# Delta stored in pieces of 256 positions and loaded two chunks at a time by the selective scan, with projection weights held only in their phase

## Chip, core and metric

The kernel runs on one core of one Trainium2 chip. The metric is the device time of one execution in microseconds (us). Before the change three runs took 11842.54, 11845.06 and 11851.63 us; the median is 11845.06 us. Two times within about 0.2% of each other can't be told apart here.

## What is computed

The input holds 8 images of 96 channels by 64 x 64 positions (L = 4096). Layer 0 is a layer norm, an input projection to 192 + 192 channels, a depthwise 3 x 3 convolution with SiLU, and then a selective scan along four orders of the positions (k = 0..3: by rows, by columns, and both backwards). Layer 1 is a linear attention and a feed-forward block. The change concerns the scan and what feeds it:

```python
x_dbl = jnp.einsum('bkdl,kcd->bkcl', xs, x_proj_w)
dts, Bs, Cs = jnp.split(x_dbl, [DTRANK, DTRANK + DSTATE], axis=2)
dts = jnp.einsum('bkrl,kdr->bkdl', dts, dt_proj_w)
delta = jax.nn.softplus(dts + dt_proj_b[None, :, :, None])
...
def step(h, t):
    u_t, d_t, B_t, C_t = t
    dA = jnp.exp(d_t[..., None] * A)
    h = dA * h + (d_t * u_t)[..., None] * B_t[:, :, None, :]
    y = jnp.einsum('bkdn,bkn->bkd', h, C_t)
    return (h, y)
```

For each k, delta is a softplus of a rank-6 projection, one number for each of 192 channels and each position; the state h has 16 numbers per channel.

## The kernel before

The images go in four pairs. Two images of 192 channels are 384 rows, held as three tiles T of 128 rows (T = 2 takes 64 rows of each image). For each pair there are three phases, and the back end of one pair runs beside the front end of the next:

1. `project` (norms, input projection), `convolve` and `gates` (SiLU, line 354) leave the scan's input `xi` in on-chip memory. Beside them run `back` and `tail` of the pair before, which end in the stores `out<-ot` (line 859).
2. `prepare` (lines 365 to 432) goes through two orders o of the positions, 8 chunks c of F = 512 positions, and the two k of each order: 32 rounds, in which the text calls one (o, c, k) a round. A round makes `pt` by three matmuls with `xw` (line 392), copies it to `S` (ScalarE, line 396), and stores the rows of B and C (`bs`, `cs`, line 398). For each T it then makes `pq` by a matmul with `dtw` (404), delta by a softplus (ScalarE, 408), `du` = delta x u (VectorE, 412), and splits delta into three bf16 parts that together hold its float32 value: part 0 on ScalarE (424), the rest on VectorE (425), part 1 on ScalarE (426), part 2 on GpSimd (427). `du` and the parts `dp` are stored to DRAM through `spread` (lines 359 and 362: one DMA for T < 2, two for T = 2). The tiles `S`, `delta`, `du`, `dp` and `rest` have three buffers each. For o = 1, GpSimd first copies `xi` into transposed tiles `u` (line 384, two buffers).
3. `scan` (lines 435 to 666) goes through 128 steps, four k with 32 chunks of TC = 128 positions. Its order is written out by hand. In step s, visit v (0 to 7), TensorE makes the exponents `da` from the delta parts `dm` and weights `aw` (`decay`, 570), two visits ahead; ScalarE takes their exp (577); GpSimd makes `dbu` = du x B (552); VectorE runs the scan (588); TensorE sums over states (606). `load(s + 1)` fetches the delta parts of the next step at visit 0, in two DMAs (478, 479) of 576 and 192 KB, whose rows are 6144 bytes.

Every DMA is issued from the one queue of SyncE (SP), in order; a DMA that must wait holds those behind it. Outside the scan a scheduler sets the order on each engine. Delta lies in DRAM as `dl`, bf16, laid out as [k][chunk of 128][part][16 rows m][24 entries e][128 positions], so that a store writes runs of 128 x 2 = 256 bytes; `du`, float32 with the same chunk, is written in runs of 512 bytes. The projection weights `winT` (input projection), `xw` and `dtw` are loaded once, at the start, into tiles that stay for the whole kernel. The lines at issue:

```python
dl: [KD, NT, 3, 16, NE, TC]                      # L889, bf16
dp = tmp.tile([128, F // TC, 3, TC], BF16)       # L419
dm[s] = wk.tile([128, NE, TC], BF16, name="dm")  # L475, two buffers
v = dl[k, c].rearrange("a m e t -> (a m) (e t)")
nc.sync.dma_start(to[0:96], v.unsqueeze(1).to_broadcast([48, 2, NE * TC]))
nc.sync.dma_start(to[96:128], v[0:32])
```

Of the kernel before, what the change touches and what calls it, by code (L numbers as in the profile page):

```python
# [19 lines left out]
DIM = 96  # L20
DI = 192
# [16 lines left out]
HQ = TC // 4  # L38
NE = 24
X0 = F - 3 * SEG  # L40
LOGEXP = "natural_log_exp_and_others"


# [8 lines left out]
def vss_attn_ffn(ctx: ExitStack, tc: tile.TileContext, a: dict):  # L52
# [33 lines left out]

    nw = load("nw", [DIM, 1])
    nb = load("nb", [DIM, 1])
    winT = load("winT", [DIM, 2 * DI])
    inb = const.tile([128, 2], F32, name="inb")  # L90
    nc.sync.dma_start(inb, a["inb"][:, 0])
    convw = load("convw", [128, 2, 9])
# [1 line left out]
    dtb = load("dtb", [128, KD, 2])  # L94


    xw = const.tile([128, KD, 3, 76], F32, name="xw")
    dtw = const.tile([128, KD, 3, 128], F32, name="dtw")
    with tc.tile_pool(name="xprep", bufs=2) as wp:
        for k in range(KD):  # L100
            for g in range(2):
                xg = wp.tile([128, 3, 2 * NS], F32, name="xg")
                nc.sync.dma_start(xg, a["xw"][k, :, g, :, 0:32])
                for b in range(2):
                    o = 32 * g + NS * b
                    nc.vector.tensor_copy(
                        xw[:, k, :, o : o + NS].rearrange("p t (n z) -> p t n z", z=2),
                        xg[:, :, NS * b : NS * b + NS].rearrange("p t (z n) -> p t n z", z=2),
                    )
            nc.sync.dma_start(xw[:, k, :, 64:76], a["xw"][k, :, 0, :, 32:44])  # L110
            nc.sync.dma_start(dtw[64:76, k], a["dtw"][k])

    def cut(name, v, *rest):

# [123 lines left out]
    def project(pair, zs, ybuf, p1, tmp, ps):  # L238

        pad = [t.rearrange("p (h w) -> p h w", w=HH + 2) for t in ybuf]  # L240
        for t in ybuf:
            nc.gpsimd.memset(t, 0.0)
        for b in range(2):
            xt = p1.tile([DIM, L], F32, name="xt", bufs=2)
            nc.sync.dma_start(xt, x[2 * pair + b])
            bst = tmp.tile([DIM, NCH, 6], F32, name="bst")
            for c in range(NCH):
                nc.vector.bn_stats(bst[:, c, :], xt[:, bass.ts(c, F)])
            mv = tmp.tile([DIM, 2], F32, name="mv")
            nc.vector.bn_aggr(mv, bst.rearrange("p c s -> p (c s)"))  # L250
            gps = ps.tile([128, F], F32, name="gps", tag="fps")
            nc.tensor.matmul(gps[:DIM, 0:1], gmat, mv[:, 0:1], start=True, stop=True)
            gm = tmp.tile([DIM, 1], F32, name="gm")
            nc.vector.tensor_copy(gm, gps[:DIM, 0:1])
            gd = tmp.tile([DIM, 1], F32, name="gd")
            nc.vector.tensor_tensor(gd, mv[:, 0:1], gm, ALU.subtract)
            gv = tmp.tile([DIM, 1], F32, name="gv")
            nc.vector.scalar_tensor_tensor(gv, gd, gd, mv[:, 1:2], ALU.mult, ALU.add)
            vps = ps.tile([128, F], F32, name="vps", tag="fps")
            nc.tensor.matmul(vps[:DIM, 0:1], gmat, gv, start=True, stop=True)  # L260
            gr = tmp.tile([DIM, 1], F32, name="gr")
            rsqrt(gr, vps[:DIM, 0:1])
            yield
            nc.vector.tensor_scalar(xt, xt, gm, gr, ALU.subtract, ALU.mult)

            for c in range(NCH):
                cs = bass.ts(c, F)
                cps = ps.tile([128, F], F32, name="cps", tag="fps")
                nc.tensor.matmul(cps[:DIM], c96, xt[:, cs], start=True, stop=True)
                sq = tmp.tile([DIM, F], F32, name="sq", bufs=1)  # L270
                nc.scalar.activation(sq, cps[:DIM], AF.Square)
                vp = ps.tile([128, F], F32, name="vp", tag="fps")
                nc.tensor.matmul(vp[:DIM], j96, sq, start=True, stop=True)
                rs = tmp.tile([DIM, F], F32, name="rs", bufs=1)
                rsqrt(rs, vp[:DIM])
                nc.vector.tensor_tensor(xt[:, cs], cps[:DIM], rs, ALU.mult)
                nc.vector.tensor_scalar(xt[:, cs], xt[:, cs], nw, nb, ALU.mult, ALU.add)
                yield

            lo = slice(64 * b, 64 * b + 64)  # L280
            for c in range(NCH):
                cs = bass.ts(c, F)
                r0 = c * ROWS
                pm = ps.tile([128, F], F32, name="pm", tag="fps")
                nc.tensor.matmul(pm, winT[:, 0:128], xt[:, cs], start=True, stop=True)
                nc.scalar.activation(
                    pad[b][:, r0 + 1 : r0 + 1 + ROWS, 1 : HH + 1],
                    pm.rearrange("p (h w) -> p h w", w=HH),
                    AF.Identity, bias=inb[:, 0:1],
                )  # L290
                pl = ps.tile([128, F], F32, name="pl", tag="fps")
                nc.tensor.matmul(pl[lo], winT[:, 128:DI], xt[:, cs], start=True, stop=True)
                nc.scalar.activation(
                    pad[2][lo, r0 + 1 : r0 + 1 + ROWS, 1 : HH + 1],
                    pl[lo].rearrange("p (h w) -> p h w", w=HH),
                    AF.Identity, bias=inb[lo, 1:2],
                )
                zt = tmp.tile([DIM, 2, F], F32, name="zt")
                for g in range(2):
                    pz = ps.tile([128, F], F32, name="pz", tag="fps")  # L300
                    nc.tensor.matmul(
                        pz[:DIM], winT[:, DI + g * DIM : DI + (g + 1) * DIM], xt[:, cs],
                        start=True, stop=True,
                    )
                    table("silu", lambda: nc.scalar.activation(
                        zt[:, g], pz[:DIM], AF.Silu, bias=inz[:, g]
                    ))
                nc.sync.dma_start(zs[b, :, :, cs].rearrange("g p l -> p g l"), zt)
                yield
# [55 lines left out]
    def prepare(xi, us, dl, du, bs, cs_):  # L365
        with ExitStack() as st:
            tmp = st.enter_context(tc.tile_pool(name="p2", bufs=3))
            ps = st.enter_context(tc.tile_pool(name="p2ps", bufs=3, space=PSUM))
            pd = st.enter_context(tc.tile_pool(name="p2pd", bufs=4, space=PSUM))

            for T in range(3):
                spread(lambda o, n: us[o : o + n], T, xi[T])
            dlv = dl.rearrange("k c a m e t -> k c a (m e) t")
            duv = du.rearrange("k c m e t -> k c (m e) t")
            for o in range(2):
                for c in range(NCH):
# [12 lines left out]
                    for k in (o, o + 2):  # L389
# [12 lines left out]
                        for T in range(3):  # L402
# [13 lines left out]
                                T, q.rearrange("p (j t) -> p j t", t=TC),  # L416
                            )

                            dp = tmp.tile([128, F // TC, 3, TC], BF16, name="dp")  # L419
                            rest = tmp.tile([128, F], F32, name="rest")  # L420
                            d, rest = [
                                t.rearrange("p (j t) -> p j t", t=TC) for t in (d, rest)
                            ]
                            nc.scalar.activation(dp[:, :, 0], d, AF.Copy)  # L424
                            nc.vector.tensor_tensor(rest, d, dp[:, :, 0], ALU.subtract)  # L425
                            nc.scalar.activation(dp[:, :, 1], rest, AF.Copy)  # L426
                            nc.gpsimd.tensor_tensor(dp[:, :, 2], rest, dp[:, :, 1], ALU.subtract)  # L427
                            spread(
                                lambda o, n: dlv[k, j, :, o : o + n]
                                .rearrange("j a p t -> p (j a) t"),  # L430
                                T, dp.rearrange("p j a t -> p (j a) t"),
                            )
# [2 lines left out]
    def scan(dl, du, bs, cs_, ys):  # L435
        with ExitStack() as st:
# [33 lines left out]
            def load(s):  # L470

                if s >= N:
                    return
                k, c, _ = steps[s]
                dm[s] = wk.tile([128, NE, TC], BF16, name="dm")  # L475
                v = dl[k, c].rearrange("a m e t -> (a m) (e t)")
                to = dm[s].rearrange("p e t -> p (e t)")
                nc.sync.dma_start(to[0:96], v.unsqueeze(1).to_broadcast([48, 2, NE * TC]))
                nc.sync.dma_start(to[96:128], v[0:32])

            def load_bc(s):
# [79 lines left out]
            def decay(p):  # L561

                if p >= 8 * N:
                    return
                s, v = divmod(p, 8)
                r, z = divmod(v, 2)
                k = steps[s][0]
                e = da[p % 3][:, 0:W6].rearrange("p (i u) -> p i u", u=SEG)[:, :, 1:]
                for i in range(NI):
                    nc.tensor.matmul(  # L570
                        e[:, i], aw[k, r][:, i, z, :], dm[s][:, NI * r + i, :],
                        start=True, stop=True,
                    )
                if p == 0:
                    table("ln", lambda: nc.scalar.activation(e, e, AF.Exp))
                else:
                    nc.scalar.activation(e, e, AF.Exp)  # L577
# [49 lines left out]
            for r in range(NR):  # L627
                load_aw(0, r)
            load(0)
            fetch(0)  # L630
            for _ in load_bc(0):
                pass
# [9 lines left out]
            for s in range(N + 2):  # L642
                for v in range(8):
# [8 lines left out]
                            sums(s - 1, f)  # L652
                    if s < N:
                        if v == 0:
                            load(s + 1)
                        if v == 1:
                            fetch(2 * s + 3)
                        if v == 5:
# [224 lines left out]
    for pair in range(npair + 1):  # L883

        new = {}
        if pair < npair:
            for name, shape, dtype in (
                ("zs", [2, 2, DIM, L], F32), ("us", [2 * DI, L], F32),
                ("dl", [KD, NT, 3, 16, NE, TC], BF16), ("du", [KD, NT, 16, NE, TC], F32),  # L889
                ("bs", [KD, NT // NB, 2 * NS, NB * TC], F32),  # L890
                ("cs", [KD, NT // NB, 2 * NS, NB * TC], F32), ("ys", [KD, 16, L, NE], F32),
                ("t1", [2, DIM, L], F32), ("tn", [2, DIM, L], F32),
# [161 lines left out]
```

## Time and profile before

| what | value |
|---|---|
| median of three runs | 11845.06 us |
| the profiled execution | 11820.4 us, its span 11818.4 us |
| mean granted TensorE clock | 0.816 |
| VectorE busy, share of the span | 8756.4 us, 74% |
| GpSimd | 7986.7 us, 68% |
| TensorE matmuls | 8675.0 us, 73% |
| ScalarE | 6900.1 us, 58% |
| data DMA: packets, bytes, share of 16 engines | 1654228, 2068.13 MB, 75.4% |
| DMA packets under 512 bytes | 962179 of 1655919 |
| first scan starts of the four pairs (line 588) | 638.8, 3533.6, 6431.7 and 9333.5 us |

The profile is one execution, recorded on the chip. In rows of a group, busy time comes first, then the mean or the min/median/max of one instruction, then the idle time of the engine ahead of it with what ended it (the releaser). A DMA packet is one contiguous run that a DMA engine moves; "share" is the mean busy share of the core's 16 DMA engines. PEclk is the clock that TensorE was granted, as a part of the full one. A float32 matmul of one source line is two TensorE instructions. The kernel repeats one pattern four times, once a pair, with the phases one after the other; shares over the whole span are an average over phases with different limits.

### The profile page before, as it was taken

The page shows a single profiled execution, that of the slowest core. Times are in us where ns is not written, and L with a number is a line of the kernel's source. Part 1 is how long each engine was busy: PE and PEld are TensorE (multiplying, and loading weights), DVE is VectorE, ACT ScalarE, POOL GpSimd, SP SyncE. Part 2 cuts the span into 40 slices and gives each one's busy share as a digit, 9 for nine tenths or more (in the row PEclk, how much of TensorE's full clock was granted, in tenths as well). Part 3 has the DMA queues.
Part 4 walks back from the last instruction along what each step waited for, and adds up shares of the span by engine and source line. Part 5 has one row for each costly group of instructions (what it writes and reads, how often), then busy time and mean ns, then how long its engine had stood idle before and what let it go on. Part 6 is the DMA issues. An engine that isn't in the chain of part 4 may idle for free. (4 is left out here: it accounts for less than half of the span.)

```text
span 11818.4 us, 387513 instructions
## 1 busy us (share of the span) xinstructions
PE 8675.0 (73%) x170112; PEld 5662.7 (48%) x170112; DVE 8756.4 (74%) x6465; ACT 6900.1 (58%) x12176; POOL 7986.7 (68%) x2770
## 2 busy tenths in 40 slices
PE   7856666779877666667986666667898666667787
PEld 2245555544225555554422555555442355555542
DVE  5489999963549999995355999999454699999922
ACT  3556666644456666664455666666445566666623
POOL 0489999960249999994025999999313699999910
PEclk8678888879768888888976888888896788888896
DMA  2988888875398888886459888888646988888862
GB/s 79 215 198 201 198 203 201 198 160 134 97 215 195 203 201 200 204 195 149 120 125 209 197 202 199 197 199 199 148 99 156 203 199 199 200 198 200 193 132 63
DMA packets 1655919, 2092.92 MB, mean 177 GB/s; under 512 B 962179, under 2 KB 1307348, under 8 KB 1651412
## 3 DMA queue, kind: packets, MB, share of 16 engines
q1 hardware_dynamic: 1654228, 2068.13, 75.4%
q8 instruction: 1335, 21.87, 0.9%
q14 instruction: 356, 2.92, 0.1%
HBM read 1604.17 MB, written 463.54 MB: 175 GB/s over the span
## 5 line engine op out<-in xcount | busy, mean ns | idle before, releaser
L588 DVE TENSOR_TENSOR_SCAN h<-da,dbu 128x774 f32<-128x774 f32 x4096 | 7028.4, 1760 | 646.5 <-ACT da L577 443.1
L552 POOL TENSOR_TENSOR dbu<-dut,bc 128x1536 f32<-128x1536 f32 x2048 | 7083.1, 3506 | 578.1 <-ACT dbu L549 478.7
L577 ACT ACTIVATE da<-da 128x768 f32<-128x768 f32 x4092 | 3254.2, 797 | 2155.9 <-PE da L570 2117.6
L606 PE MATMUL yp<-h,cw 128*32 128x48 f32 x131072 | 3145.2, 246 | 1126.0 <-issue 1110.7
L570 PE MATMUL da<-dm,aw 128*128 128x128 bf16 x24576 | 2502.0, 251 | 1447.2 <-DVE h L588 1098.1
L606 PEld LDWEIGHTS yp<-h,cw 128*32 128x32 f32 x131072 | 2548.9, 155 | 1673.2 <-issue 1408.7
L570 PEld LDWEIGHTS <-aw 128*128 128x128 bf16 x24576 | 1844.5, 111 | 1774.5 <-issue 1452.5
L506 ACT ACTIVATE cw<-bc,blk 128x512 f32<-128x512 f32 x2048 | 1472.8, 720 | 297.9 <-DMA bc<-cs 216.2
L745 POOL TENSOR_TENSOR yk<-yk 128x768 f32<-128x768 f32 x64 | 115.8, 1809 | 1268.2 <-DMA yk<-ys 1010.6
L427 POOL TENSOR_TENSOR dp<-rest,dp 128x512 bf16<-128x512 f32 x384 | 458.1, 1194 | 707.3 <-ACT dp L426 691.6
L425 DVE TENSOR_TENSOR rest<-delta,dp 128x512 f32<-128x512 f32 x384 | 301.1, 785 | 628.2 <-ACT dp L424 628.2
L404 PE MATMUL pq<-S,dtw 12*128 12x512 f32 x768 | 594.8, 882 | 140.2 <-ACT delta L408 75.3
L614 ACT ACTIVATE yev<-yp 128x384 f32<-128x384 f32 x1024 | 503.4, 492 | 243.1 <-PE yp L606 240.6
L858 POOL TENSOR_TENSOR ot<-t,y 96x512 f32<-96x512 f32 x64 | 128.1, 2002 | 612.0 <-DVE y L856 593.7
L786 DVE SCALAR_TENSOR_TENSOR g<-yc,c_onw,yrs 96x512 f32<-96x512 f32 x128 | 89.9, 742 | 483.2 <-ACT yrs L190 483.2
L404 PEld LDWEIGHTS pq<-S,dtw 12*128 12x128 f32 x768 | 162.4, 250 | 566.0 <-ACT delta L408 179.1
L426 ACT ACTIVATE dp<-rest 128x512 bf16<-128x512 f32 x384 | 241.6, 630 | 327.3 <-DVE rest L425 327.3
L672 ACT ACTIVATE nsq<-ncp 96x512 f32<-96x512 f32 x128 | 75.8, 592 | 572.8 <-PE ncp L670 559.6
L549 ACT COPY dbu<-h 128x12 f32<-128x12 f32 x1984 | 407.1, 205 | 0.0
L758 PEld LDWEIGHTS py<-ident,yk 128*24 128x24 f32 x8192 | 231.6, 108 | 241.7 <-issue 182.6
L758 PE MATMUL py<-ident,yk 128*24 128x128 f32 x8192 | 319.1, 290 | 31.5 <-DVE yk L744 25.7
L384 POOL COPY u<-xi 128x512 f32<-128x512 f32 x96 | 109.3, 1156 | 327.6 <-ACT xi L354 296.6
(136 smaller groups left out, 6684.3 us busy)
## 6 DMA issues: line engine op xcount, KB each, us to landing
dut<-du SPq DMA_DIRECT2D x1024, 768.0 KB
dm<-dl SPq DMA_DIRECT2D x512, 576.0 KB
dl<-dp SPq DMA_DIRECT2D x256, 384.0 KB
dm<-dl SPq DMA_DIRECT2D x512, 192.0 KB
ys<-yev SPq DMA_DIRECT2D x1024, 96.0 KB
du<-du SPq DMA_DIRECT2D x256, 256.0 KB
bc<-bs SPq DMA_DIRECT2D x512, 128.0 KB
bc<-cs SPq DMA_DIRECT2D x512, 128.0 KB
```

The source lines that it names most:

```text
L404: nc.tensor.matmul(pq, dtw[64:76, k, T], S[64:76], start=True, stop=True)
L425: nc.vector.tensor_tensor(rest, d, dp[:, :, 0], ALU.subtract)
L427: nc.gpsimd.tensor_tensor(dp[:, :, 2], rest, dp[:, :, 1], ALU.subtract)
L506: nc.scalar.activation(cw[i % 2][:, :, :, m, :].rearrange("p z j t -> p (z j) t"), bc[i][:, 1].rearrange("p z (j t) -> p (z j) t", j=NB), ...
L549: nc.scalar.copy(start, segs(hs[s - 1][:, :, r])[:, :, :, 1 if back else TC])
L552: nc.gpsimd.tensor_tensor(segs(t)[:, :, :, 1:], dut[g // 2][:, NI * (r % 2) : NI * (r % 2) + NI, :].unsqueeze(1) .to_broadcast([128, 2, NI ...
L570: nc.tensor.matmul(e[:, i], aw[k, r][:, i, z, :], dm[s][:, NI * r + i, :], start=True, stop=True,)
L577: nc.scalar.activation(e, e, AF.Exp)
L588: nc.vector.tensor_tensor_scan(hs[s][:, w, r][:, d], da[p % 3][:, o : o + W6][:, d], dbu[4 * s + r][:, w][:, d], 0.0, ALU.mult, ALU.add,)
L606: nc.tensor.matmul(y[32 * q : 32 * q + 32, 2 * NE * i : 2 * NE * i + 2 * NE] .rearrange("p (j r i) -> p i j r", j=2, r=NR), w[:, z, :, t], ...
L614: nc.scalar.activation(yev[s][:, :, o : o + 8, :].rearrange("p j i e -> p i j e"), y[:, 0 : 16 * NE].rearrange("p (i j e) -> p i j e", j=2 ...
L758: nc.tensor.matmul(o, yk[:, k, 4 * g + e, NE * j : NE * j + NE], ident, start=False, stop=(k + j == 4),)
```

## The change

The constant WC = 256 is new. `dl` becomes [k][chunk of 256][part][16][24][256 positions]; the tile `dp` and the stores follow, with the same bytes in runs of 512 bytes and half as many of them. The scan's tile `dm` now holds two chunks (24.6 KB a partition where it was 12.3 KB, still two buffers). It is filled in two halves: at step s, visit 0, `load(s + 2)` brings half of the 24 entries, for both chunks of a pair of steps; so each load has the bytes and the row length of before (6144 bytes, now 12288 bytes apart in DRAM), and is issued one step earlier. Ahead of the first step, `load(1)` is issued next to `load(0)`. The matmul of line 570 reads its half of the positions.

`winT` is loaded in `project`, once a pair, ahead of the images. `xw` is put together at the start as before but written to a DRAM tile `xwd`, and loaded from there at the start of each `prepare`; `dtw` is loaded there too, in one DMA. All three are thereby given back between their phases.

```diff
+WC = 256
...
-    winT = load("winT", [DIM, 2 * DI])
...
-    xw = const.tile([128, KD, 3, 76], F32, name="xw")
-    dtw = const.tile([128, KD, 3, 128], F32, name="dtw")
+    xwd = dram.tile([128, KD, 3, 76], F32, name="xwd", bufs=1)
     with tc.tile_pool(name="xprep", bufs=2) as wp:
+        xw = wp.tile([128, KD, 3, 76], F32, name="xw", bufs=1)
...
-            nc.sync.dma_start(dtw[64:76, k], a["dtw"][k])
+        nc.sync.dma_start(xwd, xw)
...
         for t in ybuf:
             nc.gpsimd.memset(t, 0.0)
+        winT = p1.tile([DIM, 2 * DI], F32, name="winT")
+        nc.sync.dma_start(winT, a["winT"])
...
+            xw = tmp.tile([128, KD, 3, 76], F32, name="xw", bufs=1)
+            nc.sync.dma_start(xw, xwd)
+            dtw = tmp.tile([128, KD, 3, 128], F32, name="dtw", bufs=1)
+            nc.sync.dma_start(dtw[64:76], a["dtw"].rearrange("k r t c -> r k t c"))
             for T in range(3):
                 spread(lambda o, n: us[o : o + n], T, xi[T])
...
-                            dp = tmp.tile([128, F // TC, 3, TC], BF16, name="dp")
+                            dp = tmp.tile([128, F // WC, 3, WC], BF16, name="dp")
...
-                                t.rearrange("p (j t) -> p j t", t=TC) for t in (d, rest)
+                                t.rearrange("p (j t) -> p j t", t=WC) for t in (d, rest)
...
-                                lambda o, n: dlv[k, j, :, o : o + n]
+                                lambda o, n: dlv[k, c * F // WC : (c + 1) * F // WC, :, o : o + n]
...
-                dm[s] = wk.tile([128, NE, TC], BF16, name="dm")
-                v = dl[k, c].rearrange("a m e t -> (a m) (e t)")
-                to = dm[s].rearrange("p e t -> p (e t)")
-                nc.sync.dma_start(to[0:96], v.unsqueeze(1).to_broadcast([48, 2, NE * TC]))
+                if s % 2 == 0:
+                    dm[s // 2] = wk.tile([128, NE, WC], BF16, name="dm")
+                e = slice(NE // 2 * (s % 2), NE // 2 * (s % 2) + NE // 2)
+                v = dl[k, c // 2, :, :, e].rearrange("a m e t -> (a m) (e t)")
+                to = dm[s // 2][:, e].rearrange("p e t -> p (e t)")
+                nc.sync.dma_start(to[0:96], v.unsqueeze(1).to_broadcast([48, 2, NE // 2 * WC]))
                 nc.sync.dma_start(to[96:128], v[0:32])
...
-                        e[:, i], aw[k, r][:, i, z, :], dm[s][:, NI * r + i, :],
+                        e[:, i], aw[k, r][:, i, z, :], dm[s // 2][:, NI * r + i, bass.ts(c % 2, TC)],
...
             load(0)
+            load(1)
             fetch(0)
...
-                            load(s + 1)
+                            load(s + 2)
...
-                ("dl", [KD, NT, 3, 16, NE, TC], BF16), ("du", [KD, NT, 16, NE, TC], F32),
+                ("dl", [KD, NT * TC // WC, 3, 16, NE, WC], BF16), ("du", [KD, NT, 16, NE, TC], F32),
```

More of the change, by code (lines that the diff above doesn't have):

```diff
@@ L566, in decay @@
                 r, z = divmod(v, 2)
-                k = steps[s][0]
+                k, c, _ = steps[s]
                 e = da[p % 3][:, 0:W6].rearrange("p (i u) -> p i u", u=SEG)[:, :, 1:]
```

## The prediction

> **What bounds the kernel now.** I read the busy shares in slices first, to see the phases, and then the two that the change touches. In the scan (500 us of it: VectorE 462.5 busy, GpSimd 465.6, DMA share 0.86, from the view by stretches) the engines are the limit, and TensorE waits for `dm` only at the phase's starts. The DMA engines are full in `prepare`, so I took its stretch by the same view, from the last gate to the end of ScalarE's work. The columns are busy us of PE, PEld, DVE, ACT, POOL, then the clock, the DMA share and GB/s.
>
> ```profile
> core 0: us, PE busy (x) PEld busy (x) DVE busy (x) ACT busy (x) POOL busy (x), PEclk, DMA share, GB/s
> 284.80:605.00 320.20, 267.10 (x382) 70.36 (x380) 141.38 (x197) 191.03 (x322) 135.84 (x117) 0.68 0.98 219
> ```
>
> The reader is to see a DMA share of 0.98 for 320 us. That alone would make the DMA the bound. The waits of ScalarE in the same stretch say something else:
>
> ```profile
> ACT dp L426 <- DVE rest L425: 81.1, 93, 2.0
> ACT S L396 <- PE pt L392: 22.9, 8, 7.8
> ACT dp L424 <- DMA dl<-dp: 20.7, 46, 1.5
> ACT dp L424 <- POOL dp L427: 2.8, 7, 0.7
> ACT delta L408 <- PE pq L404: 1.4, 4, 0.8
> ```
>
> 191.0 busy + 81.1 + 22.9 + 20.7 + 2.8 + 1.4 = 319.9 of 320.2 us. ScalarE, in its fixed order, is accounted for with no gap, and only 20.7 us is a wait for a buffer that a store of delta still reads. The largest wait is built in: it copies part 0, waits for VectorE's subtraction, and only then copies part 1.
>
> ```profile
> L424 ACT ACTIVATE dp<-delta x91: 617/629/631, 307.1 to 596.9; 128x512 bf16<-128x512 f32 x91
> L425 DVE TENSOR_TENSOR rest<-delta,dp x91: 673/692/1674, 307.8 to 598.8; 128x512 f32<-128x512 f32 x91
> L426 ACT ACTIVATE dp<-rest x91: 629/630/633, 308.5 to 599.5; 128x512 bf16<-128x512 f32 x91
> ```
>
> So two limits lie close together: the DMA, and 5% under it ScalarE's chain. The other pairs agree (321 us each; waits for `dl<-dp` of 20.4, 15.8 and 16.2 us; each also waits once, some 10.7 us, for a `cs` store behind the 6.3 MB of `us`).
>
> **Cost of a packet.** Two neighbouring 5 us stretches differ in their mix (DMA view, 405 to 410 and 410 to 415 us):
>
> ```profile
> DMA packets 3124, 1.13 MB, mean 227 GB/s; under 512 B 1981, under 2 KB 3124, under 8 KB 3124
> q1 hardware_dynamic: 3124, 1.13, 97.8%
> ...
> DMA packets 3615, 1.06 MB, mean 212 GB/s; under 512 B 3069, under 2 KB 3615, under 8 KB 3615
> q1 hardware_dynamic: 3615, 1.06, 102.9%
> ```
>
> Those under 512 B are the 256-byte runs of delta; nearly all others are 512 bytes. 1981 a + 1143 b = 0.978 x 80000 ns and 3069 a + 546 b = 1.029 x 80000 ns give a = 21.2, b = 31.8 ns. A fit over the hundred stretches of 1 us from 340 to 440 gives 20.5 and 32.6 ns; I use it. A longer run costs more; two short ones (41.0) become one of 32.6, not half.
>
> **Step 1, stores of delta.** A round stores 4608 runs of 256 bytes: 4608 x 20.5 / 16 engines = 5.90 us. After, 2304 x 32.6 / 16 = 4.69 us. With `du` (1536 x 32.6 / 16 = 3.13) and B and C (about 0.45, 1 KB runs on the same slope) a round needs 9.48 us of DMA now and 8.27 after, 1.21 less; over 32 rounds 38.7 us a pair, from about 318 (with 15 for `us`) to 280. The Trainium skill (DMA: Bandwidth & Descriptors, Specifications) promises more: below 512 bytes a transfer is not at line rate, from there it is, at about 27 GiB/s an engine. By that (an estimate from the page) a 512-byte run takes 17.7 ns, delta 2.55 us a round, and 107 us a pair are saved. But `du` is stored in 512-byte runs already, and the trace has them at 32.6 ns; the row decides.
>
> What comes out of it: ScalarE's chain stands next in line. Of the 20.7 + 20.4 + 15.8 + 16.2 = 73.1 us that it waits for `dl<-dp`, with the DMA at 280 / 306 = 0.92 of a shorter stretch, a quarter should stay (bursts: a store of 1.6 us ahead of another). I take -54 us; all of it would be -73, half -36. The drain from ScalarE's end (605.0) to the scan's first load (612.0) holds four stores of T = 2: -1 a pair, -4 (0 to -8). The ops at 424 to 427 keep their element counts; the orders of ScalarE and VectorE stay but for a few swaps, and on GpSimd each group of transposing copies moves by a few places: 0.
>
> **Step 2, the scan's loads.** In the steady scan each load has the bytes, row length and place in SP's order of before, one step earlier; half of them lose their wait for TensorE on SP (101.6 us in all at line 478), ahead of loads that are not late. No engine waits there for `dm`: 0. At the start, `load(1)` goes ahead of `dut` and `bc` on a full DMA. Now:
>
> ```profile
> 630.96 3.44 POOL L552 TENSOR_TENSOR dbu<-dut,bc 128x1536 f32<-128x1536 f32 x1 [11.96 <-DMA bc<-bs]
> 632.99 5.01 ACT L506 ACTIVATE cw<-bc,blk 128x512 f32<-128x512 f32 x8 [27.96 <-DMA cw<-cs]
> 638.79 11.73 DVE L588 TENSOR_TENSOR_SCAN h<-da,dbu 128x774 f32<-128x774 f32 x7 [18.26 <-ACT da L575]
> ```
>
> GpSimd waits for `bc`, ScalarE for `cw`, the scan for ScalarE's exp behind it. From 612 to 628 the queue moved about 4.3 MB, 270 GB/s; 0.77 MB more is 2.9 us on that chain: +3 a pair, +12. Bounds: 0 (step 0 then has one load less) and +6 (130 GB/s), so 0 to +24.
>
> **Step 3, weights.** `xw` (467 KB) comes ahead of `us` on SP. In pair 0 its buffer is free once the `zs` stores are out (last issued at 220.6; first `pt` at 283.5): 0. In pairs 1 to 3 the built order has it wait for the DMAs ahead, thus for the last output store, issued at 3170.0, landed by some 3172.5. Nearest row: two `xt` loads, 3.1 MB, issued at 32.6 and used at 42.8; so about 4 us for `xw`, there at 3176 to 3177, where the first `pt` ran at 3168.4. The first group then took 3.3 us, so `S`, now at 3179.8 behind the gates, starts up to 3 us later. `us` starts at 3178.8 as before, behind the gates. The DMA's 6.3 MB and the wait for `cs` cover most: +1 a pair, +3; without that cover +7 a pair, 21; not below 0. `winT` is 144 KB more a pair, ahead of `xt` in a stretch where TensorE is busy 48 of 50 us: 0 (at most 1 each). At the start three SP issues fewer of 0.45 us stand before `xt`, and one waiting store more: 0.
>
> **Sum.** -54 - 4 + 12 + 3 = -43 us: the profiled execution would go from 11820.4 to 11777. The runs' median lies 24.7 us higher; I carry the difference over: 11845 - 43 = 11802 us.
>
> **Rivals.**
> A, the forecast: ScalarE's chain takes over. From -73 - 8 = -81 to -36 + 24 + 21 = +9: 11764 to 11854. Chance 0.52.
> B, the DMA is the true pace-maker: the waits for TensorE and GpSimd are its echo (VectorE waits 65.9 us for `du<-du` over the kernel), and the stage shrinks by all 38.7 us. For it: share 0.98, 0.99, 0.99, 0.98 in the four pairs. Against it: the account of ScalarE has no room for more than its waits. 4 x 38.7 = 155 less, 15 given back: 11705 us. Chance 0.13.
> C, TensorE at half clock takes the place of the DMA.
>
> ```profile
> core 0: us, PE busy (x), PEclk, DMA share, GB/s
> 355.00:380.00 25.00, 25.00 (x28) 0.50 0.98 215
> 420.00:425.00 5.00, 5.00 (x12) 1.00 0.98 207
> ```
>
> At full clock 12 instructions pass in 5 us, 0.43 each: a round's twelve take 5.1 us, at half clock 10.2, while a round now takes 320 / 32 = 10.0. From 355 to 380 TensorE is busy without a gap and yet stays at 0.50. The skill (TensorE: Matmul & The Clock Gate, Part 1: The HAM clock gate) says that about 3.4 us of sustained activity release the clock; by it TensorE speeds up as soon as it lags, and C costs nothing. By the row it need not, and the waits of 73 us only change their name: -4 + 12 + 3 = +11, 11856 us, no difference. Against C: the clock does rise in places, and ScalarE waits for `pq` just 1.4 us. Chance 0.27.
> D, slower: rows of `dm` that lie 12288 bytes apart are read more slowly. A step of the scan is 14.8 us with a DMA share of 0.86, 12.7 us, of which `dm` is by bytes about 27%, 3.4 us. It decides once `dm` takes 2.1 us longer, over 60% more; each further 10% is then 0.34 x 512 steps = 174 us. At 70% more: 11845 + 174 - 43 = 11976 us. No row shows such a read; its runs of 6144 bytes are those of now. Chance 0.08.
>
> **How the numbers follow.** 0.2% is 24 us, about what a measurement can tell. Faster: most of A (0.44), B (0.13), a little of C (0.04), 0.61. Slower: D and a trace of C, 0.09. Same: 0.30. The range 11750 to 11855 holds A and most of C and leaves out D and the deeper part of B; A alone is 11764 to 11854.
>
> **What would show it.** Step 1: the fit at 340 to 440 finds hardly any packet under 512 B, with 512-byte runs at about 33 ns; `ACT dp L424 <- DMA dl<-dp` (new line 430) falls from 73 to about 20 us; the wait for `rest` stays near 80 us a pair; last gate to first `aw` load goes from 327 to some 312 us. B: 290. C: unchanged, waits for `pt` and `pq` in place of those for `dl`. Step 2: the first scan comes 27 us after the first `aw` load as now (638.8 - 612.0), plus 3; the scan's own length, 638.8 to 2533.3, stays. Step 3: first `pt` of pair 1 some 8 us later against the last output store, first softplus at most 3. I am wrong if ScalarE's waits shrink by much more than 73 us, or if the scan changes its length.

## The result, and the profile after

The changed kernel takes 11729.95 us (median of 6 runs, 11718.83 to 11756.44), the one before 11845.18 us beside it; the ratio is 0.9913, 95% interval 0.9896 to 0.9931, that is 103 us less (82 to 123; the two medians alone lie 115 apart). The forecast was 43 less, and its range ended at 11750. The profiled execution took 11732.83 us with a span of 11730.9, where before it was 11818.4: 87.5 less. All ratios are of fast runs; one run, of E2 below, fell in a slow state (12820.59 us at a granted clock of 0.592) and is left out of its ratio. Lines of `prepare` are numbered 6 higher now, those of the scan 8 higher.

The page's DMA lines first: packets under 512 bytes fell from 962179 to these 372484.

```profile
DMA packets 1362206, 2095.90 MB, mean 179 GB/s; under 512 B 372484, under 2 KB 1012997, under 8 KB 1357701
```

The stretch from the last gate to the end of ScalarE's work, pair 0, by the view by stretches (columns as in the prediction), and ScalarE's waits in it (total us, times, longest):

```profile
284.10:582.70 298.60, 250.65 (x382) 69.05 (x380) 144.86 (x197) 185.75 (x322) 132.41 (x117) 0.71 0.91 236
```

```profile
ACT dp L432 <- DVE rest L431: 85.5, 92, 2.3
ACT S L402 <- PE pt L398: 22.1, 10, 7.5
ACT dp L430 <- DMA dl<-dp: 2.7, 5, 0.8
ACT delta L414 <- PE pq L410: 1.4, 4, 0.8
ACT dp L430 <- POOL dp L433: 0.7, 1, 0.7
```

The reader is to see 320.2 become 298.6 us, the DMA share fall from 0.98 to 0.91, and the waits for `dl<-dp` go. The wait for `rest` stays, 4 us longer. ScalarE's two copies hardly changed: their medians are 618 and 630 ns (629 and 630 before). VectorE's subtraction reads

```profile
L431 DVE TENSOR_TENSOR rest<-delta,dp 128x512 f32<-128x512 f32 x96 | 81.1, 846 | 137.0 <-ACT dp L430 136.9
```

Over the whole kernel its mean rose from 785 to 845 ns. Alone it takes 691 ns in both kernels, and some 950 when a GpSimd operation runs beside it, which happened 139 times of 384 before and 229 times after.

The same two 5 us stretches as in the prediction, 405 to 410 and 410 to 415, hold hardly a packet under 512 bytes now:

```profile
DMA packets 2486, 1.28 MB, mean 255 GB/s; under 512 B 123, under 2 KB 2486, under 8 KB 2486
...
q1 hardware_dynamic: 2486, 1.28, 99.5%
...
DMA packets 2742, 1.37 MB, mean 274 GB/s; under 512 B 69, under 2 KB 2742, under 8 KB 2742
...
q1 hardware_dynamic: 2742, 1.37, 100.8%
```

0.995 x 80000 / 2486 = 32.0 ns a packet, and 29.4 in the other: near the 32.6 ns of the forecast, and far from the 17.7 ns estimated from the line rate of the Trainium skill (DMA: Bandwidth & Descriptors, Specifications).

At the scan's start (timeline of pair 0; the first `aw` load at 587.6) every step is later against that load:

```profile
610.02 3.43 POOL L560 TENSOR_TENSOR dbu<-dut,bc 128x1536 f32<-128x1536 f32 x1 [15.41 <-DMA bc<-bs]
612.14 5.01 ACT L514 ACTIVATE cw<-bc,blk 128x512 f32<-128x512 f32 x8 [29.46 <-DMA cw<-cs]
...
617.94 8.41 DVE L596 TENSOR_TENSOR_SCAN h<-da,dbu 128x774 f32<-128x774 f32 x5 [21.71 <-ACT da L583]
```

617.9 - 587.6 = 30.4 us from the first load to the first scan, 26.8 before (all from the trace's unrounded times).

Over the four pairs, in us, profiled execution before and after:

| stretch | before | after | difference |
|---|---|---|---|
| start or scan's end to the last gate | 2210.7 | 2201.3 | -9.4 |
| last gate to the end of ScalarE's `dp` copies | 1290.8 | 1205.3 | -85.5 |
| from there to the first `aw` load | 27.7 | 19.9 | -7.8 |
| first `aw` load to the first scan | 101.9 | 115.0 | +13.1 |
| the scans | 7607.6 | 7611.6 | +4.0 |
| last scan to the end | 579.7 | 577.8 | -1.9 |

The 85.5 us do not come evenly. Cut at the 17th copy of `S`, where the first order of the positions ends, `prepare` reads, over the four pairs:

| part of `prepare` | before: us a pair, DMA share | after: us a pair, DMA share |
|---|---|---|
| first order | 143 to 147, 0.99 to 1.00 | 129 to 130, 0.96 to 0.98 |
| second order | 176 to 179, 0.97 to 0.98 | 170 to 173, 0.86 to 0.87 |

About 16 us a pair come off in the first order, where the DMA stays nearly full, and only some 5 in the second.

### The profile page after: what moved, and what is told of

The parts are those of the page before. It is cut to its first block, busy times and chain, and to the rows that moved or that the text cites. A ratio compares the mean times of both kernels' runs of the same rounds, so it can differ in the third digit from the quotient of the medians.

```text
span 11730.9 us, 387292 instructions
## 1 busy us (share of the span) xinstructions
PE 8603.2 (73%) x170112; PEld 5660.7 (48%) x170112; DVE 8762.0 (75%) x6465; ACT 6884.1 (59%) x12176; POOL 7973.1 (68%) x2770
## 5 line engine op out<-in xcount | busy, mean ns | idle before, releaser
L433 POOL TENSOR_TENSOR dp<-rest,dp 128x512 bf16<-128x512 f32 x384 | 448.9, 1170 | 608.5 <-ACT dp L432 590.5
L410 PE MATMUL pq<-S,dtw 12*128 12x512 f32 x768 | 508.7, 770 | 114.8 <-ACT delta L414 61.0
L767 PE MATMUL py<-ident,yk 128*24 128x128 f32 x8192 | 313.7, 287 | 29.2 <-DVE yk L753 21.6
```

The costliest lines, as they stand in the source:

```text
L410: nc.tensor.matmul(pq, dtw[64:76, k, T], S[64:76], start=True, stop=True)
L767: nc.tensor.matmul(o, yk[:, k, 4 * g + e, NE * j : NE * j + NE], ident, start=False, stop=(k + j == 4),)
```

## The experiments

Two theories stood at the outset. **D**: the shorter DMA time of the stores did it, and the DMA had been the pace of `prepare`. **W**: a good part comes from the weights, by their residency or the place of their loads. A third, **S**, says what stopped the gain at 21 us a pair: ScalarE's chain with the wait for `rest` in it. Ratios are to the kernel before, timed on the same chip in the same rounds; `prepare` and scan are means of the four pairs of one profile.

| run | ratio (95% interval) | prepare | start | scan |
|---|---|---|---|---|
| before, first profile | | 322.7 | 25.5 | 1901.9 |
| after, first profile | 0.9913 (0.9896 to 0.9931) | 301.3 | 28.7 | 1902.9 |
| E5 before again | 1.0010 (0.9996 to 1.0025) | 327.7 | 24.9 | 1905.4 |
| E6 after again | 0.9914 (0.9894 to 0.9933) | 302.1 | 28.2 | 1908.8 |
| E1 weights alone | 0.9976 (0.9965 to 0.9987) | 329.7 | 25.1 | 1895.4 |
| E9 weights alone again | 0.9959 (0.9944 to 0.9974) | 328.8 | 25.3 | 1891.1 |
| E12 weights, places kept | 0.9984 (0.9968 to 0.9999) | 329.6 | 25.2 | 1910.8 |
| E13 weights, asked ahead | 0.9986 (0.9970 to 1.0003) | 334.0 | 28.3 | 1899.4 |
| E2 after, runs of 256 bytes | 1.0011 (1.0000 to 1.0022) | 323.5 | 28.7 | 1903.6 |
| E10 stores alone | 1.0261 (1.0244 to 1.0278) | 301.0 | 26.5 | 2014.5 |
| E3 after, `load(1)` late | 0.9914 (0.9897 to 0.9930) | 301.3 | 25.5 | 1910.7 |
| E4 after, part 1 on VectorE | 0.9954 (0.9938 to 0.9971) | 308.9 | 28.1 | 1903.6 |
| E7 after, part 1 behind | 0.9898 (0.9876 to 0.9920) | 294.4 | 28.1 | 1904.6 |
| E8 before, part 1 behind | 0.9993 (0.9982 to 1.0004) | 325.0 | 24.8 | 1906.5 |
| E11 as E7, six buffers | 0.9898 (0.9882 to 0.9915) | 292.8 | 29.2 | 1914.1 |
| E14 after, asked later | 0.9617 (0.9594 to 0.9640) | 301.4 | 28.5 | 1827.3 |
| E15 as E7, asked later | 0.9601 (0.9579 to 0.9624) | 295.3 | 28.5 | 1822.6 |

**E5 and E6, the ground.**

> The kernel before, unchanged, profiled a second time beside the other three. It gives the size of the scatter of each stage between executions. All theories: ratio 1.000; if the first stretch up to the first gates takes 268 to 273 us here (285 in the first profile), that difference belongs to the chip or the hour and not to the weights' part; if the scan takes 7600 us or more again, the 26 us less that the scan took with the weights' part alone may be real.

> The changed kernel, unchanged, timed and profiled on the same chip as the other three. All theories: ratio 0.990 to 0.993, prepare 298 to 303 us a pair, start 28 to 30 us. It is the ground on which the two reordered kernels of this call are judged.

They repeat, and show the scatter of one profile: `prepare` 322.7 and 327.7 us a pair, a scan 3 to 6 us. The first stretch took 284.2 us in E5, but 269 to 285 in others, old and new alike: no effect of the change.

**E1 and E9, the weights alone.** `winT`, `xw` and `dtw` loaded for their phase, nothing else of the diff.

> The kernel before with only the weights moved to their phase; delta is stored in 128-position pieces and loaded a chunk at a time, as before. Theory D (the pieces of delta did it): the weights' part costs nothing that shows, since the wait for xw ends before the gates do: before +0 to +5 us, prepare 320 us a pair, ratio to before 0.9995 to 1.0010. Rival W (a good part of the gain is the residency or the place of the weight loads): at least a third of the 103 us is here, ratio 0.997 or below.

> The weights' part alone, timed and profiled a second time. Theory F (the first measure of 28 us less was real: some 11 us of it is in the stretches between a scan's end and the next gates, which were 3.6 us a pair shorter in all kernels with the moved weights): ratio 0.997 to 0.9985. Rival N (scatter of the runs and nothing more): 0.9985 to 1.001. The prepare of 344 us that its first profile showed in the last pair should not come back: 321 to 326 us a pair.

No theory holds as it was put: 0.9976 lies between D and W, and 0.9959 is below both ranges of E9 and reaches W's. There is a gain, 28 us (15 to 41) and 49 us (31 to 66), but it isn't in `prepare`: the scans are shorter, 7581.6 and 7564.5 us in all where the resident weights have 7607.6, 7621.7 and 7625.9 (E8). What I had expected not to return did: single pairs of `prepare` of 340 to 346 us, in E1, E9, E12 and E13. Such a pair (E1, pair 3), by stretches and ScalarE's waits:

```profile
8945.10:9288.60 343.50, 292.65 (x381) 75.54 (x379) 143.44 (x197) 190.74 (x322) 139.70 (x119) 0.62 0.93 209
```

```profile
ACT S L401 <- PE pt L397: 46.2, 9, 7.5
```

A clock of 0.62 and 46 us of waiting for `pt`, at a DMA share of 0.93: this is how rival C, TensorE at a low clock, would look, some 20 us longer than the other pairs. The first pair of E5 is a milder one (332.9 us, clock 0.62, 37 us for `pt`). It came only with stores of 256 bytes, and in none of the changed kernel's eight pairs; what brings it on was not tested.

**E2, the runs alone undone.** The changed kernel, with delta in DRAM in pieces of 128 and a tile of two chunks filled a chunk at a time.

```diff
-dp = tmp.tile([128, F // WC, 3, WC], BF16, name="dp")
+dp = tmp.tile([128, F // TC, 3, TC], BF16, name="dp")
...
-dm[s // 2] = wk.tile([128, NE, WC], BF16, name="dm")
+dm[s // 2] = wk.tile([128, 2, NE, TC], BF16, name="dm")
```

> The changed kernel with one thing undone: delta lies in DRAM in pieces of 128 positions again, so that prepare stores it in runs of 256 bytes; the tile of two chunks, the two loads at the head of each scan, their sizes and their times stay as changed. Theory D: prepare goes back to about 320 us a pair (+80 us in all), the drain to 6.9 us, the scan's start stays at 28 to 30 us, so the time is that of before plus the 13 us of the start: 11850 to 11865 us, ratio to before 1.0005 to 1.0015. Rival W or a rival in which the two-chunk load does it: it stays within 30 us of the changed kernel, ratio 0.994 or below.

D holds: 1.0011 is 13 us more than before (0 to 26), which fits the 13 us that the start is longer. By stretches and waits, pair 1:

```profile
3171.40:3496.10 324.70, 282.36 (x380) 74.14 (x378) 144.60 (x197) 191.02 (x322) 137.69 (x119) 0.64 0.98 222
```

```profile
ACT dp L432 <- DVE rest L431: 83.0, 94, 2.0
...
ACT dp L430 <- DMA dl<-dp: 15.4, 37, 1.5
```

So the longer runs are worth 0.9913 / 1.0011, some 116 us, and the rest of the change costs about 13. As the weights alone gain 28 to 49, the two-chunk tile with its earlier asking would take about 41 to 62 back. That is a difference between runs, and right only if the parts add up.

**E10, the stores alone.** The kernel before, weights resident, delta stored in pieces of 256; the scan still loads one chunk at a time, now in runs of 256 bytes and with three DMAs in place of two.

```diff
-v = dl[k, c].rearrange("a m e t -> (a m) (e t)")
...
-nc.sync.dma_start(to[0:96], v.unsqueeze(1).to_broadcast([48, 2, NE * TC]))
+v = dl[k, c // 2].rearrange("a m e t -> (a m) e t")[:, :, bass.ts(c % 2, TC)]
...
+for z in range(2):
+    nc.sync.dma_start(to[z:96:2], v)
```

> The kernel before with the stores' part alone: prepare writes delta in pieces of 256 positions (runs of 512 bytes); the weights stay where they were, the scan still loads a chunk at a time, which it now reads in runs of 256 bytes, with three DMAs in place of two. Theory D: prepare 300 to 303 us a pair, drain 5 us, start 25 to 27 us; the scan's loads take 3072 packets of 256 bytes a chunk at 20.7 ns over 16 engines, 4.0 us of DMA time, about 1 us a chunk more than now beside 0.85 of a chunk's 30 us that the DMA engines are busy. If that hides: 85 to 95 us less than before, ratio 0.992 to 0.993. If the scan pays it: up to 64 us back, ratio 0.997. Rival (the moved weights are needed for the gain): 0.998 or above with prepare back at 320.

`prepare` has the whole gain, 301.0 us a pair, without the weights' part. The scan lost far more than the 64 us: 110 a pair. By stretches, `prepare` and scan of pair 0:

```profile
273.10:571.10 298.00, 252.91 (x382) 69.23 (x380) 145.15 (x197) 185.83 (x322) 132.77 (x117) 0.71 0.91 237
602.20:2619.00 2016.80, 1344.97 (x38646) 1128.12 (x38645) 1754.25 (x1024) 1246.12 (x2277) 1765.35 (x523) 0.77 0.92 186
```

A DMA share of 0.92 against 0.85, and TensorE now waits 514 us for `dm` in the four scans (5 before). That the DMA engines had been free for 15% of the time did not hide the reads. (The third DMA was not tried apart from the short runs.) The two-chunk tile keeps the rows of the loads long while the stores get their longer runs.

**E8 and E7, who sets the pace.** ScalarE's order is fixed so that a tile's second copy stands behind the next tile's softplus and first copy; `dp` has four buffers. The wait for `rest` is then gone in both kernels.

```diff
+if late:
+    late.pop()()
+def finish(dp=dp, rest=rest, k=k, c=c, T=T):
+    table("softplus", lambda: nc.scalar.activation(dp[:, :, 1], rest, AF.Copy))
...
+late.append(finish)
```

> The kernel before with the same fixed order of ScalarE and four buffers for dp, delta still stored in 256-byte runs. Theory D with S (before, the DMA engines are the pace at a share of 0.98, and ScalarE only waits for them): prepare stays within 4 us of 322 a pair, ratio to before 0.998 to 1.001; ScalarE's wait for rest turns into waits for dl<-dp. Rival A of the prediction (both share the pace, ScalarE's own chain is a limit of its own close behind): 5 us a pair or more come off, ratio 0.9975 or below.

> The changed kernel with ScalarE's order in prepare fixed so that the copy of a tile's second part stands behind the softplus and the first copy of the next tile; dp has four buffers. The same work on the same engines; ScalarE no longer waits 85.5 us a pair for VectorE's rest. Theory S (in the changed kernel ScalarE's chain, that wait in it, is the pace of prepare): prepare falls to the next limit, the DMA engines at a share of 0.98: 0.91 x 302 / 0.98 = 280 us a pair, 80 us less than the changed kernel, about 11650 us, ratio to before 0.983 to 0.986. Rival P (TensorE, busy 257 of 302 at a clock of 0.70, or the DMA engines at 0.91, are as fast as they get): prepare 297 to 303 us, ratio 0.990 to 0.993.

ScalarE's waits, E8 pair 2 and then E7 pair 2:

```profile
ACT dp L425 <- DMA dl<-dp: 97.7, 74, 3.1
...
ACT dp L431 <- DVE rest L426: 3.1, 3, 1.5
```

```profile
ACT dp L431 <- DMA dl<-dp: 66.6, 73, 2.6
...
ACT dp L437 <- DVE rest L432: 1.4, 2, 1.0
```

In the kernel before, the 82 us of waiting for `rest` go, the waiting for the stores rises from 16 to 98, and the pair stays at 325 at a DMA share of 0.99 or more: the DMA was the pace, and ScalarE's chain only waited in other places for it. In the changed kernel 7 to 8 us a pair come off (and 1.7 go back in the drain), so ScalarE's chain was a limit there; but it stops at 294, with `dl<-dp` back at 58 to 68 us, between the 280 of theory S and the 297 to 303 of rival P. By the times, 0.9898 against 0.9914 in E6 cannot be told apart.

**E11, six buffers for `dp`.**

> The changed kernel with ScalarE's order fixed as in the run before, and six buffers for dp instead of four. There prepare took 294 us a pair, ScalarE waited 60 us a pair for dl<-dp at a DMA share of 0.94. Theory B6 (it is the latency of a store in the queue that holds the buffers): prepare 280 to 286 us, DMA share 0.97 or more, 30 to 50 us less than with four buffers. Rival T (the DMA engines give no more with these transfers; a deeper queue only lengthens the wait): 291 to 296 us, the wait goes to another row.

292.8, in rival T's range: deeper buffers gain nothing that can be told from E7. That the DMA sets this limit, as T has it, is not shown. In the first order its share is 0.98 to 0.99; in the second it is 0.87 to 0.90, and there ScalarE waits longest for `pt`, 32 to 40 us a pair, with TensorE at a clock of 0.63 to 0.67. What holds `prepare` at 293 stays open.

**E4, the second copy on VectorE.**

```diff
-nc.scalar.activation(dp[:, :, 1], rest, AF.Copy)
+nc.vector.tensor_copy(dp[:, :, 1], rest)
```

> The changed kernel with delta's second bf16 part copied by VectorE instead of ScalarE (the same bytes to the same places). Theory S (with the shorter stores the pace of prepare is ScalarE's chain, busy 186.5 us and waiting 85.5 us for VectorE's rest in 302; the DMA engines are busy 0.91 of it): ScalarE loses some 55 us of work and the wait for rest, and prepare falls until the DMA engines are full again, 0.91 x 302 / 0.98 = 280 us a pair: 80 us less than the changed kernel, about 11650 us, ratio to before 0.983 to 0.986. Rival M (the DMA engines are still the pace at a share of 0.91): within 15 us of the changed kernel, ratio 0.990 to 0.9925.

Both missed: 308.9 us. The operations of VectorE and GpSimd got longer (here over the whole kernel; 845 and 1170 ns in the changed kernel), VectorE has 201 us of copies more (384 of 523 ns), and ScalarE waits for VectorE instead:

```profile
L433 POOL TENSOR_TENSOR dp<-rest,dp 128x512 bf16<-128x512 f32 x384 | 511.6, 1333 | 609.9 <-DVE dp L432 316.0 <-issue 116.9 <-DMA cs<-S 111.1
L431 DVE TENSOR_TENSOR rest<-delta,dp 128x512 f32<-128x512 f32 x384 | 434.9, 1134 | 284.0 <-ACT dp L430 284.0
L414 ACT ACTIVATE delta<-pq,c_dtb 128x512 f32<-128x512 f32 x384 | 263.8, 687 | 535.4 <-DVE rest L431 439.9 <-PE pq L410 89.1 <-DVE dp L432 3.6
```

**E3, `load(1)` behind the first diagonals.**

> The changed kernel with the second half of the first delta tile asked for behind the first chunk's diagonal loads instead of ahead of them. If the 13 us that the start of the scan lost are the time of that transfer in front of the first chunk's other operands: start back from 28 to 30 us to 25 to 27 us a pair, 10 to 13 us less than the changed kernel in all, about 11718 us (ratio to before 0.9892 to 0.9905). If the loss is in something else (the wider rows, two DMAs more): no change from the changed kernel.

The start came back (25.5 us a pair, 13 less in all): the second load is the cause of the later start. The time did not show it, but 13 us are less than the interval of the ratio (some 20 us either way). Start and scan together took 7744.6 us, against 7726.6 and 7748.1 in the two profiles of the changed kernel; whether the later start costs time at the end of the scan stays open.

**E12 and E13, why the weights and the asking move the scan.** E12 adds to E1 a tile of 11.3 KB that nothing reads, so that the scan's tiles lie where they lay; E13 adds `load(1)` at the head, `load(s + 2)` and a third one-chunk buffer.

> The weights' part alone, with 11.3 KB a partition held by a tile that nothing reads, the bytes that the resident weights took, so that the scan's tiles lie where they lay before. Theory L (the place of the tiles makes the scan 45 us shorter): the scan goes back to 7608 to 7626 us, ratio 0.998 to 1.000. Rival Q (something else in the moved loads does it): scan 7564 to 7582 us, ratio 0.995 to 0.9975.

> The weights' part alone with delta still in one-chunk tiles, three of them, asked for two chunks ahead as in the changed kernel (two loads at the head). Theory H (the time of asking costs the scan): start 28 to 30 us a pair, scan 7610 to 7640 us, ratio 1.000 to 1.002, like the run with 256-byte stores and two-chunk tiles. Rival V (the two-chunk tile itself costs): start up by 3 us a pair but scan 7564 to 7582 us, ratio 0.9965 to 0.9985.

E12's scan went to 7643.4 us, which speaks for the place of the tiles, but its ratio overlaps that of E1. E13's scan of 7597.5 us lies between the theories, and its ratio of 0.9986 a little above V's range. Neither is settled: in six profiles with the changed kernel's scan (after, E3, E4, E6, E7, E11) the total runs from 7611.6 to 7656.4 us.

**E14 and E15, asking later.** In the changed kernel, and in E7:

```diff
-if v == 0:
-    load(s + 2)
 if v == 1:
     fetch(2 * s + 3)
+if v == 4:
+    load(s + 2)
```

> The changed kernel with each half tile of delta asked for half a chunk later (at the fifth piece of a chunk in place of the first). Theory H: the scan loses part of its 50 us, 7570 to 7610 us, 20 to 50 us less than the changed kernel, ratio 0.987 to 0.990. Rival V: no change, 0.990 to 0.9925. If a half tile comes too late, the scan grows instead.

> The run with ScalarE's order fixed (prepare 294 us a pair) and delta asked for half a chunk later: both edits that may help, together. If they add up: 20 us from prepare with its drain, 20 to 50 us from the scan, ratio 0.985 to 0.988. If the later asking does nothing: 0.989 to 0.990.

Far beyond all expectation: 76 us a scan, and with E7's order 0.9601, median 11398.87 us against 11869.57. This is the version that beats both kernels. Where it comes from shows in two rows of the page. First the changed kernel, then E14 (VectorE's scans, then TensorE's matmuls of `yp`):

```profile
L596 DVE TENSOR_TENSOR_SCAN h<-da,dbu 128x774 f32<-128x774 f32 x4096 | 7026.9, 1760 | 665.2 <-ACT da L585 450.9
...
L614 PE MATMUL yp<-h,cw 128*32 128x48 f32 x131072 | 3145.5, 246 | 1091.3 <-issue 1075.2
```

```profile
L596 DVE TENSOR_TENSOR_SCAN h<-da,dbu 128x774 f32<-128x774 f32 x4096 | 7022.3, 1759 | 366.3 <-ACT da L585 219.2
...
L614 PE MATMUL yp<-h,cw 128*32 128x48 f32 x131072 | 3036.3, 241 | 627.6 <-issue 612.8
```

VectorE idles 299 us less, nearly the scans' whole gain of 303; TensorE idles 462 less in gaps for which the profile names no releaser. The granted clock in the four scans is 0.87 to 0.88 where it was 0.82 to 0.84, and the matmuls of line 614 are busy 109 us less. Whether the shorter gaps raised the clock or the clock has a part of its own in the gain is not separated. Whether the same edit helps the kernel before, with one-chunk tiles and half the lead, wasn't tried.

## Why the prediction was wrong

**The step that failed is "ScalarE's chain stands next in line ... I take -54 us", and under it the reading of the account.** That busy time and waits of ScalarE fill 319.9 of 320.2 us was taken to mean that only its waits for `dl<-dp` could go. But an engine with a fixed order is always accounted for without a gap, whoever sets the pace. E8 settled it: ScalarE freed of 80 us a pair gained nothing, so before the change the DMA was the pace, as rival B said. Measured, `prepare` lost 85.5 us where -54 was forecast: 31.5 of the 44.5 us by which the profiles' difference of 87.5 exceeds the forecast of 43.

The term itself was right: `dl<-dp` fell from 73.1 to 14.4 us, -58.7. What the forecast had put at nothing were ScalarE's other rows, which shrank with the full DMA, summed over the four pairs: the wait for GpSimd's part 2 (its link to the DMA is argued), 22.1 to 2.1; the wait for `cs<-S`, 32.1 to 8.4; and 16.5 us less busy time of ScalarE, since two of its operations with no wait between them overlap in the records by some 95 ns, and there were more of these. Against these `rest` rose by 15.6, `pt` by 8.6 and three small rows by 9. Together that is -86, against -85.5 measured.

**Rival B** had the mechanism and not the size: 38.7 us a pair, where 21 came. In the first order, where the DMA stayed nearly full, 16 of its 19.4 us came; in the second only 5. What stopped it is at least in part what the forecast had put in its place, ScalarE's chain, at 302 us and not at 306: E7 and E11 take 7 to 9 us more off `prepare`. They end at 293 to 294 and not at the 280 of the packet sum, for a reason that stays open. So B's cause was real and A's stop was real in part, and the truth lay between their numbers.

**The drain** fell by 7.8 us (forecast 4). **The start** rose by 13.1 (12): E3 shows that the second load is its cause. **The scan** kept its length, +4 (0), and the weights, put at +3, gain 28 to 49. The sum of these two parts was right, +15 forecast and +13 (0 to 26) in E2, but by luck: a shorter scan with the weights moved and, by the difference of the runs, a longer one with the two-chunk tile cancel out. That no engine waits for `dm` did not make the load's place in the queue free, as E14 shows.

**Packets**: 32.6 ns forecast for 512 bytes, 29.4 to 32.0 measured; the choice of the row over the skill's line rate stands. **Rival C** did not come in the changed kernel: the clock in `prepare` is 0.70 to 0.71 (0.64 to 0.68 before). **Rival D** is refuted for rows 12288 bytes apart: E2, whose rows follow one another, has scans of 7614.5 us in all, the changed kernel 7611.6 and 7635.4. It would have been right of runs of 256 bytes (E10).

## What to carry over

When a DMA share stands at 0.98, a complete account of an engine's waits does not make that engine the limit; take the engine's largest wait away in an experiment. When the next limit is sized, count every wait that a full queue can echo in, not only the one with the store's name. Cut a phase where its work changes: here the DMA stayed nearly full in one half and not in the other. And where the engines are busy 92% and the DMA 85%, the place of a large load in the queue can be worth more (here 3.0% on top of the change, 0.9617 against 0.9914) than the bytes that a change saves.

## What the runs showed of the hardware

Most of TensorE's unexplained gaps in the scan end just behind a packet of the instruction queue. In the changed kernel's scans there are 464 gaps of over 0.7 us ahead of matmuls of line 614, 1047 us in all, and 458 of them end 1.1 to 2.0 us after a packet of the instruction queue q8 has landed (of times drawn at random 15% do). Before, it was 474 of 479; with the later asking 311 gaps are left, 584 us. These packets are 16 KB each, some 1215 in the four scans, and the profile counts them among the 16 DMA engines' packets as it does the data. That TensorE lacks instructions there, and that their fetch waits behind a large load, is argued from this, not shown: the packets themselves take as long in both kernels (1.30 us, median), and E10, with the fuller DMA, has only 201 such gaps, 444 us. That the place of the loads moves the gaps' total from 1047 to 584 us is shown by E14.

VectorE and GpSimd slow each other in operations with two inputs in SBUF (the on-chip memory): in E7, where line 419 (`du`) falls beside GpSimd's subtraction, it takes 1328 ns with `u` as input where it took 702, and the subtraction 1349 where it took 1170. The Trainium skill (SBUF — State Buffer, Who interferes with whom) has a port pair that the one holds and the other waits for, which fits. In E4 `rest` and the subtraction are longer in the same way; how much of E4's loss this is, and how much VectorE's added copies, was not separated.
